# Four graph-attention layers over 16 graphs: adjacency masks as transposed byte pairs, and another order of the first and last layers

## The chip, the cores and the metric

The kernel runs on one core of one Trainium2 chip. The metric is device time in microseconds from start to end of one execution; the median of five runs is given with the lowest and the highest. The profile is of one further execution.

## The reference, cut to what matters

There are 16 graphs of 1024 nodes with 256 features, and for each a symmetric adjacency of 1024 x 1024 int32 (0 or 1, the diagonal set). Four attention layers follow each other, each on the normalised, rectified features, each added to the features:

```python
h = jnp.maximum(_layernorm(x, axis=-1), 0.0)
x = x + _L0_gnn_ref(h, adj, W, a)          # layers 1, 2 and 3 alike, with weights of their own

# _L0_gnn_ref, 4 heads of 64:
h = (x @ W).reshape(Bq, Nq, H, HD).transpose(0, 2, 1, 3)
s1 = jnp.einsum('bhnd,hd->bhn', h, a1)
s2 = jnp.einsum('bhmd,hd->bhm', h, a2)
e = jax.nn.leaky_relu(s1[:, :, :, None] + s2[:, :, None, :], 0.2)
e = jnp.where(adj[:, None, :, :] == 0, -jnp.inf, e)
out = jnp.einsum('bhnm,bhmd->bhnd', jax.nn.softmax(e, axis=-1), h)
```

Layers 0 to 2 have four heads; layer 2 also adds a bias, rectifies, adds its own `h` and normalises each head (gamma, beta). Layer 3 has one head of 256.

## The kernel before

`tile_gnn_stack_kernel` runs `fast_path` and then a general path, which is entered only if a check at the end of the fast path found data outside its assumptions (adjacency entries other than 0 and 1 among them). For the data of this case only the fast path does the work, and all that follows is about it.

**The work on a tile.** The exponential of a leaky ReLU of a sum is written as a product of factors and a maximum, so that it needs no exponential for each pair of nodes. The factors are made once for a layer (`fac`). A tile is one head and one block of 128 neighbours j against all 1024 nodes. For each tile ACT computes `r = relu(scale * rows + bias)` into PSUM (`weigh`; `rows` holds a factor of all 1024 nodes, the same on each partition), DVE computes `p = (r + base) * mask` into SBUF (`cover`, a scalar_tensor_tensor with the uint8 mask), and PE sums `po += p^T v` with `v` the projected features and a column for the denominators (`gather`, 16 matmuls for each half of the nodes). `ps_r` has two buffers of 128 x 1024 float32, there are TILES = 12 buffers for `p`, and two for `po`. With four heads and eight blocks a layer ("unit") has 32 tiles; there are 48 such units, named (graph, layer) below. Layer 3 is handled by `last_layer` and `last_sums`: 16 halves of two blocks each by ACT and DVE, then 8 blocks of sums on PE, each followed by an output transfer from `y`.

**Around a unit.** `prepare` takes the statistics (`st` on DVE, `rs` on POOL), `normal` scales the features (`hn` on POOL), turns them on PE and rectifies them (`hT`, ACT), `project` multiplies by the weights (`wa`) and copies the result (`v`, ACT). Then come the greatest scores (`mx`, `top`, `diag`, `c`), the factors (`fac`), and `rows`: the factor is turned on PE, copied by DVE (`row`), written to DRAM by SP (`line`), and read back to all partitions once for each head (`rows`, or `rows_one` for layer 3). There are ROWS = 3 buffers, so a row is requested when the head three places earlier has been weighed. After the sums, `evacuate` takes `po` to `att` and `finish` scales it, for layer 2 adds the bias and normalises, and adds it to `x_cur`, all element-wise steps on POOL and reductions on DVE.

**The masks.** `load` brings a graph's features (SP, one transfer) and its adjacency. For graphs 0 and 1 (TURNED = 2) `fetch` casts blocks of 128 rows to bf16 on their way into SBUF (issued by POOL), PE transposes them, ACT squares the result into the mask with a sum (`edges`), and PE sums the untransposed block. For the other 14 graphs POOL issues four casting transfers of 256 rows each from int32 to bf16 in DRAM (`near`), and SP then eight transposing transfers, one for each block of 128 columns, into two `raw` buffers. For each block `far_edges` has ACT go over `raw` twice: once to square it into the uint8 mask, once to copy it, each with a sum. At the end the two kinds of sums are compared; they are equal only if all entries are 0 or 1.

**The order.** Instructions are issued under a manual schedule. The planner (`while True` at line 1180) keeps a time for each engine (`Plan`, with costs of its own), offers the next `weigh`, `cover` and `gather` and all open jobs (generators that yield the engine of their next step and a condition), and on the engine that is free first takes, among what is ready within NEAR = 60 ns of the earliest, what is due first. Each engine then runs its instructions strictly in that order, SP its transfers too. The order of units is a rule (line 1129): it interleaves the graphs so that a unit is normally at least two places behind the one whose result it needs. It ends (13,2), (14,1), (15,0), (14,2), (15,1), (15,2). Loads begin EARLY = 110 tiles ahead of a graph's first unit, and layer 3 of a graph half a unit after its layer 2 has begun.

**The start.** Before the planner's loop, SP issues the transfers of all weights and attention vectors, DVE folds the vectors into the weights (16 products and 16 reductions), and only then do the planner's instructions begin on SP and DVE.

Of the kernel before, what the change touches and what calls it, by code (L numbers as in the profile page):

```python
# [9 lines left out]
F32 = mybir.dt.float32  # L10
BF16 = mybir.dt.bfloat16
I32 = mybir.dt.int32
# [364 lines left out]
TURNED = 2  # L377
# [10 lines left out]
M_PE = 300.0  # L388
# [10 lines left out]
LARGE = ("v_", "x_cur", "mask", "sums", "greatest", "p0", "p1", "p2", "p3", "p4", "p5", "p6", "p7", "p8", "p9", "r_", "po", "pl", "pp", "row", "hT", "raw", "inv")  # L399
# [81 lines left out]
def fast_path(  # L481
# [39 lines left out]
    NQ = NB // QUAD  # L521
# [11 lines left out]
    ident_b = const.tile([P, P], BF16, name="ident_b")  # L533
    make_identity(nc, ident_b)
# [6 lines left out]


    sums = const.tile([P, 2, G * NB], F32, name="sums")

    ones_b = const.tile([P, 1], BF16, name="ones_b")
    nc.vector.memset(ones_b, 1.0)

    def rows(src: bass.AP, offset: int, dims: list, name: str, pool, **kw):

        t = pool.tile([P] + [n for _, n in dims], F32, name=name, **kw)  # L550
        nc.sync.dma_start(t, bass.AP(tensor=src.tensor, offset=src.offset + offset, ap=[[0, P]] + dims))
        return t
# [3 lines left out]
    for k in range(KC):  # L556
        f = slice(k * P, (k + 1) * P)
        nc.sync.dma_start(wa[0][:, k, :, :HO], w_0[f, :].rearrange("p (h e) -> p h e", h=H))
        nc.sync.dma_start(wa[1][:, k, :, :HO], w_1[f, :].rearrange("p (h e) -> p h e", h=H))
        nc.sync.dma_start(wa[2][:, k, :, :HO], w_2[:, f, :].rearrange("h p e -> p h e"))  # L560
    with (
        tc.tile_pool(name="fold", bufs=2) as prep,
        tc.tile_pool(name="ps_w", bufs=2, space=bass.MemoryType.PSUM) as ps_w,
    ):
        w3_in = prep.tile([P, KC, F], F32, name="w3_in", bufs=1)
        nc.sync.dma_start(w3_in, w_3.rearrange("(c p) f -> p c f", p=P))
        for k in range(KC):
            pw = ps_w.tile([P, 512], F32, name="pw")
            for c in range(KC):
                nc.tensor.transpose(pw[:, c * P : (c + 1) * P], w3_in[:, c, k * P : (k + 1) * P], ident)  # L570
            nc.vector.tensor_copy(wa[3][:, k, 0, :F], pw[:, :F])
        for side in range(2):
            r = [
                rows(a_0, side * HO, [[2 * HO, H], [1, HO]], "a0", prep),
                rows((a_src_1, a_dst_1)[side], 0, [[HO, H], [1, HO]], "a1", prep),
                rows((a_src_2, a_dst_2)[side], 0, [[T * HO, H], [1, HO]], "a2", prep),
                rows(a_3, side * F, [[F, 1], [1, F]], "a3", prep),
            ]
            for layer in range(LAYERS):
                w = F // HEADS[layer]  # L580
                for k in range(KC):
                    prod = prep.tile([P, HEADS[layer], w], F32, name=f"prod{HEADS[layer]}")
                    nc.vector.tensor_mul(prod, wa[layer][:, k, :, :w], r[layer])
                    nc.vector.tensor_reduce(wa[layer][:, k, :, w + side], prod, AX.X, ALU.add)
    bias_r = rows(bias_2, 0, [[1, F]], "bias_r", const)
    gamma_r = rows(gamma_2, 0, [[1, F]], "gamma_r", const)
    beta_r = rows(beta_2, 0, [[1, F]], "beta_r", const)
# [7 lines left out]
    ps_r = ctx.enter_context(tc.tile_pool(name="ps_r", bufs=2, space=bass.MemoryType.PSUM))  # L595
# [23 lines left out]

    def load(g: "Graph"):  # L620

        yield "SP", lambda: (g.b < LIVE or layers[g.b - LIVE][0].g.done) and (
            g.b == 0 or layers[g.b - 1][0].g.loaded
        )
        g.x = graphs.tile([P, NB, F], F32, name="x_cur")
        sp.dma_start(g.x, x[g.b].rearrange("(c p) f -> p c f", p=P))
        g.here = plan.now
        g.mask = graphs.tile([P, NB, N], U8, name="mask")
        if g.b < TURNED:
            for nb in range(2):  # L630
                yield "POOL", None
                fetch(g, nb)
            return
        near = dram.tile([N, N], BF16, name="near", bufs=1)
        for k in range(0, N, N // 4):
            yield "POOL", None
            pool.dma_start(near[k : k + N // 4, :], adj[g.b, k : k + N // 4, :])
        there = plan.now + FETCH
        for j in range(NB):
            yield "SP", lambda: there if j < 2 else len(g.turned) > j - 2 and g.turned[j - 2]  # L640
            raw = work.tile([P, N], BF16, name="raw", bufs=2)
            sp.dma_start(raw, near[:, j * P : (j + 1) * P], transpose=True)
            add(g.until, far_edges(g, j, raw), plan.now)

    def far_edges(g: "Graph", j: int, raw: bass.AP):

        yield "ACT", None
        at = g.b * NB + j
        act.activation(g.mask[:, j, :], raw, AF.Square, accum_out=sums[:, 0, at : at + 1])
        g.left -= 1  # L650
        if not g.left:
            g.loaded = plan.now
        yield "ACT", None
        act.activation(raw, raw, AF.Copy, accum_out=sums[:, 1, at : at + 1])
        g.turned.append(plan.now)

    def fetch(g: "Graph", nb: int):
        raw = work.tile([P, N], BF16, name="raw", bufs=2)
        pool.dma_start(raw, adj[g.b, nb * P : (nb + 1) * P, :])
        add(g.until, edges(g, nb, raw), plan.now)  # L660

    def edges(g: "Graph", nb: int, raw: bass.AP):

        yield "PE", free_bank
        at = g.b * NB + nb
        pt, k = bank(BF16)
        for j in range(NB):
            pe.transpose(pt[:, j * P : (j + 1) * P], raw[:, j * P : (j + 1) * P], ident_b)
        yield "ACT", None
        act.activation(  # L670
            g.mask[:, :, nb * P : (nb + 1) * P],
            pt.rearrange("p (j n) -> p j n", j=NB),
            AF.Square,
            accum_out=sums[:, 0, at : at + 1],
        )
        drop(k)
        g.left -= 1
        if not g.left:
            g.loaded = plan.now
        yield "PE", free_bank  # L680
        pc, k = bank()
        for j in range(NB):
            pe.matmul(pc[:, 0:1], raw[:, j * P : (j + 1) * P], ones_b, start=(j == 0), stop=(j == NB - 1))
        yield "DVE", None
        dve.tensor_copy(sums[:, 1, at : at + 1], pc[:, 0:1])
        drop(k)
        if nb + 2 < NB:
            yield "POOL", None
            fetch(g, nb + 2)
# [27 lines left out]
    def project(e, i: int):  # L717

        u = e.u
        width = u.n * (u.w + 2)  # L720
        yield "PE", free_bank
        pv, slot = bank()
        for k in range(KC):
            for c in range(0, P, P // 2):
# [565 lines left out]
```

## Time and profile before

| what | value |
|---|---|
| median of 5 runs | 3102.45 us (3101.4 to 3104.15) |
| the profiled execution | 3100.49 us, span 3098.5 us, mean granted clock 0.972 |
| PE busy, idle | 2756.0 us (89%), 342 us |
| DVE busy | 2636.0 us (85%) |
| ACT busy | 2526.8 us (82%) |
| POOL busy | 1596.5 us (52%) |
| DMA queues, share of 16 engines | 20.2% (SP's), 5.5% (POOL's) |

A page gives the busy time of each engine, the span in 40 slices of about 77 us, and the costliest groups of instructions: engine, operation, output <- inputs, number, then busy time with the mean of one, then the idle time of that engine just before them and what ended it. All instructions of the planner bear line 459, a helper's, so groups are told apart by their tiles. PE is matrix multiplication, PEld its weight loads (they overlap), SP issues transfers. A busy PE need not be at its peak, since the ends of matmuls are modelled. Idle time on an engine costs something only where the others wait too.

### The profile page before, as it was taken

The page shows a single profiled execution, that of the slowest core. Times are in us where ns is not written, and L with a number is a line of the kernel's source. Part 1 is how long each engine was busy: PE and PEld are TensorE (multiplying, and loading weights), DVE is VectorE, ACT ScalarE, POOL GpSimd, SP SyncE. Part 2 cuts the span into 40 slices and gives each one's busy share as a digit, 9 for nine tenths or more (in the row PEclk, how much of TensorE's full clock was granted, in tenths as well). Part 3 has the DMA queues.
Part 4 walks back from the last instruction along what each step waited for, and adds up shares of the span by engine and source line. Part 5 has one row for each costly group of instructions (what it writes and reads, how often), then busy time and mean ns, then how long its engine had stood idle before and what let it go on. Part 6 is the DMA issues. An engine that isn't in the chain of part 4 may idle for free.

```text
span 3098.5 us, 130601 instructions
## 1 busy us (share of the span) xinstructions
PE 2756.0 (89%) x58885; PEld 2259.7 (73%) x58885; DVE 2636.0 (85%) x4062; ACT 2526.8 (82%) x3425; POOL 1596.5 (52%) x2288
## 2 busy tenths in 40 slices
PE   3889899899899989999899999989999999999875
PEld 2777677778787777778777777877777777777663
DVE  2878999788898989899898989989898898999672
ACT  2889898887979798897979889897988979887652
POOL 2433765463654727555372655637365463745441
PEclk8999999999999999999999999999999999999997
DMA  4331311413242331323224132321313232111010
GB/s 114 84 81 48 94 54 56 96 54 84 69 107 55 86 78 50 88 69 102 57 66 93 55 88 69 89 69 59 89 57 97 61 91 76 42 42 53 19 43 22
DMA packets 197079, 217.35 MB, mean 70 GB/s; under 512 B 131360, under 2 KB 166944, under 8 KB 195616
## 3 DMA queue, kind: packets, MB, share of 16 engines
q1 hardware_dynamic: 192416, 175.35, 20.2%
q0 software_dynamic: 4096, 33.56, 5.5%
q8 instruction: 463, 7.59, 1.0%
q14 instruction: 104, 0.85, 0.1%
HBM read 195.43 MB, written 46.99 MB: 78 GB/s over the span
## 4 chain that ended last, share of the span: by engine, by line
ACT 36%; DVE 25%; PE 23%; issue 7%; POOL 4%; DMA 4%; SPq 0%; DVEq 0%; ACTq 0%; POOLq 0%
ACT r L459 24%; DVE p L459 15%; PE pp L459 12%; PE po L459 11%; ACT mask L459 3%; ACT raw L459 3%; ACT v L459 2%; ACT hT L459 2%; DVE att L459 2%; DMA raw<-near 2%; DVE st L459 2%; POOL rs L459 2%; DVE s L459 1%; ACT att L459 1%; POOL hn L459 1%
## 5 line engine op out<-in xcount | busy, mean ns | idle before, releaser
L459 ACT ACTIVATE r<-rows,fac 128x1024 f32<-128x1024 f32 x1536 | 1754.3, 1154 | 291.9 <-DVE p L459 278.2
L459 PE MATMUL po<-v,p 128*64 128x65 f32 x49152 | 1667.7, 226 | 195.2 <-DVE p L459 124.1
L459 PEld LDWEIGHTS po<-v,p 128*64 128x64 f32 x49152 | 1586.0, 140 | 341.8 <-DVE p L459 135.2
L459 DVE SCALAR_TENSOR_TENSOR p<-r,mask 128x1024 f32<-128x1024 f32 x1024 | 1222.9, 1218 | 188.4 <-ACT r L459 146.2
L459 DVE SCALAR_TENSOR_TENSOR p<-r,fac,mask 128x1024 f32<-128x1024 f32 (+1 forms) x768 | 817.5, 1099 | 70.2 <-ACT r L459 62.8
L459 PE MATMUL pp<-wa,hT 128*64 128x264 f32 (+1 forms) x4096 | 528.9, 392 | 9.4 <-ACT v L459 5.0
L459 POOL TENSOR_TENSOR att<-att,inv 128x512 f32<-128x512 f32 x128 | 133.5, 1043 | 722.8 <-DVE inv L459 678.4
L459 PE MATMUL pp<-v_one,p 128*64 128x257 f32 x4096 | 491.0, 383 | 12.4 <-DVE p L459 10.1
L459 PEld LDWEIGHTS pp<-v_one,p 128*64 128x64 f32 x4096 | 284.4, 138 | 136.0 <-issue 11.7
L459 PEld LDWEIGHTS pp<-wa,hT 128*64 128x64 f32 x4096 | 267.1, 138 | 143.0 <-ACT v L459 13.0
L459 POOL TENSOR_SCALAR hn<-x_cur,rs 128x256 f32<-128x256 f32 x512 | 282.3, 566 | 21.8 <-PE pp L459 17.7
L459 PE MATMUL pp<-ident,hn 128*128 128x128 f32 x1024 | 184.6, 300 | 86.3 <-POOL hn L459 65.7
L459 POOL TENSOR_TENSOR x_cur<-att,x_cur 128x512 f32<-128x512 f32 x192 | 227.7, 1186 | 15.1
L459 ACT ACTIVATE r<-rows_one,fac 128x512 f32<-128x512 f32 x256 | 198.1, 780 | 33.9 <-DVE p L459 18.4
L459 PEld LDWEIGHTS pp<-ident,hn 128*128 128x128 f32 x1024 | 112.0, 146 | 146.2 <-POOL hn L459 107.8
L459 DVE BATCH_NORM_STATS2 st<-x_cur 128x6 f32<-128x256 f32 x512 | 179.1, 409 | 18.2 <-DMA x_cur<-in_x_dram 9.9
L459 ACT ACTIVATE hT<-pp 128x512 f32<-128x512 f32 x256 | 149.6, 595 | 50.7 <-PE pp L459 49.3
L459 POOL TENSOR_TENSOR att<-att,bias_r 128x512 f32<-128x512 f32 x64 | 75.8, 1185 | 181.8 <-DVE att L459 104.3
L459 ACT COPY v<-pp 128x264 f32<-128x264 f32 x384 | 142.8, 383 | 29.9 <-PE pp L459 28.1
L459 POOL TENSOR_TENSOR v<-v,fac 128x512 f32<-128x512 f32 x128 | 140.1, 1115 | 29.6 <-ACT fac L459 29.6
L459 POOL TENSOR_TENSOR att<-att,s 128x512 f32<-128x512 f32 x128 | 133.5, 1043 | 10.3
L459 ACT ACTIVATE mask<-raw 128x1024 uint8<-128x1024 bf16 x112 | 117.4, 1048 | 19.2 <-DMA raw<-near 19.2
(83 smaller groups left out, 1637.2 us busy)
## 6 DMA issues: line engine op xcount, KB each, us to landing
rows<-line SPq DMA_DIRECT2D x192, 512.0 KB, 4.0
near<-in_adj_dram POOLq DMA_DIRECT2D x56, 512.0 KB, 8.5
x_cur<-in_x_dram SPq DMA_DIRECT2D x16, 1024.0 KB, 9.7
out_dram<-y SPq DMA_DIRECT2D x128, 128.0 KB, 1.8
rows_one<-line SPq DMA_DIRECT2D x16, 512.0 KB, 4.1
raw<-in_adj_dram POOLq DMA_DIRECT2D x16, 256.0 KB, 4.4
raw<-near SPq DMA_TRANSPOSE x112, 3.7
wa<-in_L_gnn_W_dram SPq DMA_DIRECT2D x6, 128.0 KB, 7.1
```

Source lines behind the costliest of these rows:

```text
L459: r = call(*a, **k)
```

## The change

What it does:

- The adjacency is cast from int32 to uint8 in DRAM (four transfers a graph, one for each 256 nodes), and the bytes are taken two at a time as a 16-bit element, so that four transposing transfers bring a whole graph into SBUF: partition p holds the nodes 2p and 2p + 1 of each 256. They go straight into `g.edges`; the mask of block j is every second byte. Nodes are permuted accordingly in the loads of x and in the output.
- ACT no longer makes the masks. All graphs take this way; the path over PE for graphs 0 and 1 is gone.
- The check reads the int32 adjacency again, 8 pieces of 128 x 1024 a graph, and ACT goes over each once, with `(a - 0.5)^2` summed: 0.25 for each 0 or 1 (`looked_over`, `look`).
- Weights are loaded and folded as jobs of the planner, layer by layer (`weights`), behind graph 0's features. The first unit may also use the wide PSUM buffers for its preparation, and its first head's `rows` are made by 16 matmuls on PE and one copy (`direct`); the same for graph 15's layer 3.
- The last nine units get an order written out. Layer 3 of graph 13 is held until 100 tiles before the end of all tiles (HOLD). The last unit's heads 2 and 3 are finished on DVE (BY_DVE = 2). Graph 15's layer 3 sums its first four blocks side by side in four PSUM buffers.
- Some copies may go to either ACT or DVE; with DVE_MORE = 1e9 they go to ACT. The planner's margin after PE (M_PE) goes from 300 to 400 ns.

The core of the diff:

```diff
-TURNED = 2
+BY_DVE = 2
+HOLD = 100
+DVE_MORE = 1e9
+DIRECT = 1
+DELAY = 12000.0
...
-M_PE = 300.0
+M_PE = 400.0
...
+    def weights(layer: int):
+
+        yield "SP", lambda: layers[0][0].g.x is not None and (DELAY * layer + 1.0)
+        p, slot = numerators()
...
+        for c in range(2):
+            sp.dma_start(a[:, c], rows(*vectors[c]))
...
+        for c in range(2):
+            for k in range(KC):
+                yield "DVE", lambda: landed
+                dve.tensor_mul(prod, wa[layer][:, k, :, :w], a[:, c])
+                dve.tensor_reduce(wa[layer][:, k, :, w + c], prod, AX.X, ALU.add)
+        leave(slot, 2)
+        folded[layer] = plan.now
...
-        sp.dma_start(g.x, x[g.b].rearrange("(c p) f -> p c f", p=P))
+        sp.dma_start(
+            g.x.rearrange("p (q c) f -> p q c f", c=2), x[g.b].rearrange("(q p c) f -> p q c f", p=P, c=2)
+        )
         g.here = plan.now
-        g.mask = graphs.tile([P, NB, N], U8, name="mask")
...
-        near = dram.tile([N, N], BF16, name="near", bufs=1)
-        for k in range(0, N, N // 4):
+        g.edges = graphs.tile([P, NQ2, N], BF16, name="mask")
+        near = dram.tile([N, N // 2], BF16, name="near", bufs=2)
+        to = near.bitcast(U8).rearrange("(q c p) m -> q c p m", c=2, p=P)
+        of = adj[g.b].rearrange("(q p c) m -> q c p m", p=P, c=2)
+        for q in range(NQ2):
             yield "POOL", None
-            pool.dma_start(near[k : k + N // 4, :], adj[g.b, k : k + N // 4, :])
+            pool.dma_start(to[q], of[q])
         there = plan.now + FETCH
-        for j in range(NB):
-            yield "SP", lambda: there if j < 2 else len(g.turned) > j - 2 and g.turned[j - 2]
-            raw = work.tile([P, N], BF16, name="raw", bufs=2)
-            sp.dma_start(raw, near[:, j * P : (j + 1) * P], transpose=True)
-            add(g.until, far_edges(g, j, raw), plan.now)
...
+        for q in range(NQ2):
+            yield "SP", lambda: there
+            sp.dma_start(g.edges[:, q, :], near[:, q * P : (q + 1) * P], transpose=True)
+        g.loaded = plan.now + 3000.0
+        add(g.until + 2 * STEPS, looked_over(g), plan.now)
+
+    def looked_over(g: "Graph"):
+
+        of = adj[g.b].rearrange("(p r) m -> p (r m)", p=P)
+        for k in range(0, N * N // P, N):
+            yield "SP", lambda: len(looks) < 2 or (looks[-2] or False)
+            raw = work.tile([P, N], I32, name="raw", bufs=2)
+            sp.dma_start(raw, of[:, k : k + N])
+            looks.append(None)
+            add(g.until + 2 * STEPS, look(raw, len(looks) - 1), plan.now)
+
+    def look(raw: bass.AP, k: int):
         yield "ACT", None
-        at = g.b * NB + j
-        act.activation(g.mask[:, j, :], raw, AF.Square, accum_out=sums[:, 0, at : at + 1])
...
-        act.activation(raw, raw, AF.Copy, accum_out=sums[:, 1, at : at + 1])
...
+        act.activation(raw, raw, AF.Square, bias=-0.5, accum_out=sums[:, k : k + 1])
+        looks[k] = plan.now
+
+    def mask(g: "Graph", j: int, at: slice = slice(None)):
+
+        e = g.edges[:, j // 2, :].bitcast(U8).rearrange("p (n c) -> p n c", c=2)
+        return e[:, at, j % 2]
...
+        direct = u is main[0] or n == 1 and u.g.b >= G - DIRECT
+        if direct:
+
+            yield "PE", free_wide
+            pr, k = wide_bank()
+            for b in range(NB):
+                for m in range(0, P, P // 2):
+                    of = u.fac[:, 0, 0, b : b + 1].to_broadcast([P, P // 2])
+                    pe.matmul(pr[m : m + P // 2, b * P : (b + 1) * P], of, ident)
+            yield "DVE", None
+            over = units.tile([P, N], F32, name="rows", bufs=ROWS)
+            dve.tensor_copy(over, pr)
...
-            dve.scalar_tensor_tensor(p, r, base, u.g.mask[:, j, :], ALU.add, ALU.mult)
+            dve.scalar_tensor_tensor(p, r, base, mask(u.g, j), ALU.add, ALU.mult)
...
+        eng, name = (dve, "DVE") if u is main[-1] and h >= H - BY_DVE else (pool, "POOL")
...
+        if u is layers[-1][-1]:
+
+            yield "PE", lambda: there(0) and all(opened) and all(t is not None for t in banks) and max(there(0), *banks, *opened[-2:])
+            free = [bank(), bank(), (ps_o.tile([P, 512], F32, name="po"), None), (ps_o.tile([P, 512], F32, name="po"), None)]
...
+    if G > 5:
+
+        b = G - 4
+        order = [(b, 2), (b + 1, 1), (b + 2, 0), (b + 3, 0), (b + 1, 2), (b + 2, 1), (b + 3, 1), (b + 2, 2), (b + 3, 2)]
+        main[-9:] = [layers[i][k] for i, k in order]
...
+                if b >= G - 2:
+                    u.held = main[b - G - 1] if len(main) > 2 else None
+                if b == G - 3:
+                    u.gate = len(main) * STEPS - HOLD
...
+    for layer in range(LAYERS):
+        begins.append((-(10**6), weights(layer), turn[0, min(layer, 2)] + (layer > 2) * STEPS - 5 * STEPS // 4))
```

## The prediction

> **What bounds the kernel now.** I read the page first: busy shares, slices, costliest groups.
>
> ```profile
> PE 2756.0 (89%) x58885; PEld 2259.7 (73%) x58885; DVE 2636.0 (85%) x4062; ACT 2526.8 (82%) x3425; POOL 1596.5 (52%) x2288
> ...
> PE   3889899899899989999899999989999999999875
> ```
>
> No engine is the bound alone: three of them are within 230 us of each other, and a tile passes from ACT (`r`) to DVE (`p`) to PE (`po`) through only two `r` buffers. So time goes where one engine makes the next one wait, and where there is too little to do: the first slice has PE at 3 tenths and the last at 5. Next I asked for busy time by stretches, for the two ends beside a middle stretch.
>
> ```profile
> 1500.00:1800.00 300.00, 281.10 (x6039) 230.13 (x6037) 271.11 (x414) 260.00 (x350) 171.00 (x233) 0.99 0.28 74
> ...
> 2900.00:2950.00 50.00, 34.60 (x444) 23.04 (x438) 20.04 (x56) 20.49 (x40) 12.55 (x25) 0.89 0.12 39
> ```
>
> Columns after the length: PE, PEld, DVE, ACT, POOL busy, clock, DMA share, GB/s. In the middle DVE is busy 90%; in 2900 to 2950 only 40%. Then the waits between 300 and 2880 us, and the operations by form:
>
> ```profile
> DVE p L459 <- ACT r L459: 157.6, 263, 3.5
> ...
> L459 ACT ACTIVATE raw<-raw 128x1024 bf16<-128x1024 bf16 x112 | 117.5, 1049 | 0.6
> L459 ACT ACTIVATE mask<-raw 128x1024 uint8<-128x1024 bf16 x112 | 117.4, 1048 | 19.2 <-DMA raw<-near 19.2
> ```
>
> DVE waits 158 us for `r` in the middle, and ACT spends 235 us (with its accumulator reads, 191 ns each, 278) on the two passes a mask block. To see whether these are linked I went through the timeline of ACT and DVE and put each idle time of DVE that ended with an `r` under "edge" when a mask or raw pass lay in it or ended within 1.2 us before it: 79 us of the 158 us, in 88 of 263 waits. The last view is the timeline, at the start and the end:
>
> ```profile
> 26.06 0.38 SPq L459 DMA_DIRECT2D x_cur<-in_x_dram  x1
> 31.43 2.71 DVE L459 BATCH_NORM_STATS2 st<-x_cur 128x6 f32<-128x256 f32 x8 [5.45 <-DMA x_cur<-in_x_dram]
> 57.00 0.27 DVE L459 TENSOR_REDUCE mx<-v 128x8 f32<-128x64 f32 x1 [5.66 <-ACT v L459]
> 69.52 2.15 ACT L459 ACTIVATE r<-rows,fac 128x1024 f32<-128x1024 f32 x2 [2.30 <-DMA rows<-line]
> ...
> 3024.08 2.71 DVE L459 BATCH_NORM_STATS2 st<-x_cur 128x6 f32<-128x256 f32 x8 [6.01 <-POOL x_cur L459]
> 3043.04 0.18 DVE L459 TENSOR_REDUCE mx<-v_one 128x2 f32<-128x16 f32 x1 [16.26 <-ACT v_one L459]
> 3051.56 10.82 ACT L459 ACTIVATE r<-rows_one,fac 128x512 f32<-128x512 f32 x14 [5.25 <-DMA rows_one<-line]
> ```
>
> The first `r` comes at 69.5 us. The loads of the weights stand first on SP and their folding first on DVE, so graph 0's features are requested only at 26 us. At the end the last graph's fourth layer runs alone: 89 us from its last `po` sum at 3010 to 3099, in which PE is busy 50.
>
> **The change, part by part.** The sum is against the profiled execution, 3100.5 us (span 3098.5); the median of the runs is 3102.5.
>
> *Edge passes.* ACT loses 224 passes with their reads, 224 x (1.05 + 0.19) = 278 us, and 16 PSUM ones, 16 x 1.21 = 19; it gains 128 `look` passes over int32. No row shows ACT reading int32; the same size from bf16 is 1.05 and from f32 rows into PSUM 1.15, plus 0.19: 1.24 to 1.34 each, 159 to 172 us. I take 1.24, since source and target lie in SBUF as in the bf16 row: ACT is 138 us lighter. Little of that is on the path; what is, are the DVE waits. Half as many passes should leave half of the 79 us: **-40**. Ends: 0, if each look costs what two passes cost now, and -79, if looks only fill idle time. They have a later due time (two units after the masks), but ACT is picked by who is ready first, so a look starts in any gap over 60 ns and can still hold back an `r`; hence the middle.
>
> *The wait at 174 us.* ACT sits 9.2 us behind a mask pass whose transposed block has not landed (175 to 183 us, DVE and PE empty too). Masks no longer pass through ACT, and DVE needs that one some 100 tiles later: **-8** (0 to -9).
>
> *Head.* SP now issues graph 0's features first. They landed in 5.3 us alone and in 12.2 beside other traffic; with 4 MB of adjacency moving beside them I take 10: statistics at 11 instead of 31.4. From `st` to `mx` took 25.6 us here, with edge work between, and 19.0 undisturbed (3024.1 to 3043.0): `mx` at 30. Layer 0's four weight loads queue behind x and fold in 4 x 0.84 = 3.4 us of DVE while POOL normalises, hidden; if they land 10 us late, they cost that much. `mx` to `fac` 4.2, then 16 matmuls and one 1.1 us copy in place of the trip through DRAM (61.9 to 69.5 now): about 3. First `p` at 38 to 39, not 70.7: -32. But DVE also needs the mask, which before came through PE in pieces: four casts (a middle batch kept the DMA engines busy from 1261 to 1276, 15 us), then four transposes of 3.7 us to landing, so 34 us alone and 44 with x and weights beside. I take 44: **-25**, ends 0 and -32.
>
> *Order of the last units.* Now (15,1) is followed at once by (15,2), which needs its result: DVE does 16.2 of 45 us between 2905 and 2950 where 89% would be 40. With (14,2) between them this goes: **-20** (0 to -24).
>
> *The end.* Heads 2 and 3 of the last unit finish on DVE: seven operations of 1.04 to 1.19 us on POOL become about 0.7 to 0.86 (DVE's `att` rows of 512): -3. Rows by matmul instead of line and rows_one (3046.6 to 3051.6): -3. Four blocks summed side by side instead of in turn: PE stays at 256 x 0.109 = 28 us, so -2. The fourth layers of graphs 13 and 14 are held back to fill the gap: such a layer is some 17 us of DVE (16 x 0.74 and 8 x 0.65), which leaves the full stretch; part of it lies there already (64 `pp` matmuls at 3009.7): **-10** (0 to -19). Together **-18**.
>
> *At nothing.* The mask read with a step of two bytes: `p` is 1218 and 1277 ns for 1024 elements with a step of one; the row with a wide step, `mx<-v`, takes 259 ns for 64 elements, `top` 269 for 128. I take 0. If it cost 5%, 1792 x 0.06 = 107 us would eat the gain; no reason excludes that, and none speaks for it. Loads of int32 for the looks: 128 x 512 KB; a 1 MB load took 5.3 us, so about 2.6 us each, 340 us of all engines, while 48 transposes go; a DMA share near 26% goes to 30%. They are covered by rows being requested two heads ahead. On SP, each issue is 0.3 us and the wait for a free `raw` stands before rows, as transposes did before. The larger PE margin moves the whole order: +-15.
>
> Sum: 40 + 8 + 25 + 20 + 18 = 111; 3100.5 - 111 = 2989.5, about **2992** on the scale of the median.
>
> *A rule against it.* The row: a batch of casts, each 256 rows in one run, kept about 0.8 of the 16 DMA engines busy for 15 us, 48 engine-us each. The Trainium skill ("DMA: Bandwidth & Descriptors", Why a DMA increments its semaphore by 16 and not by 1) says that a transfer is spread over the largest count up to 16 that divides the slowest dimension of both patterns; the new source pattern begins with a dimension of 2, so by the page two engines would carry each cast. By an estimate from that, a cast takes 24 us; if the four take different pairs the masks come 10 us later at the start (2999), if they share one pair, 96 us, and the second rival below holds. No row here shows such a pattern.
>
> **The rivals.** *First: only the ends gain.* Looks fall into the same places as the passes did, and graph 0's mask comes as late as 70 us: 3100.5 - 8 - 38 = 3054. For it: ACT idles 258 us in the middle behind DVE, and a 1.24 us look fits into few of these gaps (365 of them, 0.7 us mean). Against it: half the passes are gone.
>
> *Second, slower: SP is held by the casts.* The four transposes stand on SP 15 us after the casts were planned and wait there in order; behind them are `rows`, `line`, x and the output. A row is requested two heads ahead; a graph takes 182 us for its 12 heads, so 30 us, less 4.0 to landing: 26 us of cover. So nothing happens until a batch takes 15 + 26 = 41 us; beyond that each graph from the third on loses the rest, 14 times. At 49 us the gain is gone; at 60 us it is 14 x 19 = 266, and with -111 gives 3256. Against: 15 us in the row, with less to write now (1 MB, not 2).
>
> *Third: the passes are not the cause.* If DVE's waits near mask passes go to other ACT work, and the tail order meets a new wait, gains and the 107 us of a slower mask read cancel: within 6 us of 3102.
>
> **How the numbers follow.** The forecast (2940 to 3040) has 0.68; the first rival (3040 to 3090) 0.18; the second 0.09; the third 0.03; still faster, with all upper ends (3100 - 179 = 2921), 0.02. The range 2940 to 3075 takes in the first rival's 3054 and a bit beyond, and leaves out under 0.2. 0.2% (6 us) is about what this kernel's measurement can tell from no change; so faster 0.88, same 0.03, slower 0.09.
>
> **What would show it.** Right: first `r` at 36 to 45 us; ACT busy near 2390; DVE's wait for `r` near 115 in the middle; `p` still 1.22 and 1.28 us; no stretch of 45 us after 2800 with DVE under half before the last unit ends; 64 transposes. Wrong: ACT `r` waiting for `rows`, SP waiting long for `near`, `p` above 1.3 us, or DVE waiting on transposed masks at the start.

## The result, and the profile after

The changed kernel takes 3109.79 us (median of 32 runs, 3099.64 to 3119.51) against 3102.59 us before (54 runs, 3094.97 to 3110.21). The ratio is 1.0021, 95% interval 1.0015 to 1.0027: slower by 0.2%, where 111 us less were forecast. The profiled execution took 3111.57 us, its span is 3109.7, so 11.2 us more span than before.

The page after, with the rows that answer to those of before. The last two columns of a DMA row are the size of one transfer and the median time from its issue to its landing; a queue's row has packets, MB and share.

```profile
PE 2764.9 (89%) x58692; PEld 2258.5 (73%) x58692; DVE 2645.5 (85%) x4062; ACT 2415.5 (78%) x3201; POOL 1609.7 (52%) x2262
...
PE   3879789899998999899999989999999989989867
...
q0 software_dynamic: 132096, 17.24, 7.9%
...
L463 ACT ACTIVATE raw<-raw 128x1024 int32<-128x1024 int32 x128 | 134.9, 1054 | 57.2 <-DMA raw<-in_adj_dram 56.9
...
near<-in_adj_dram POOLq DMA_DIRECT2D x64, 256.0 KB, 27.0
```

ACT's busy time is 111 us lower (the times of its instructions add up to 142 us less, where 138 were forecast), and DVE's work is the same, but nothing got shorter by it. The row to notice is the last: a cast lands after 27.0 us. Before it was this, for twice the bytes written:

```profile
q0 software_dynamic: 4096, 33.56, 5.5%
...
near<-in_adj_dram POOLq DMA_DIRECT2D x56, 512.0 KB, 8.5
```

The two stretches after (columns as before):

```profile
1500.00:1800.00 300.00, 280.74 (x5862) 226.81 (x5862) 270.16 (x416) 247.15 (x325) 160.64 (x223) 0.99 0.31 84
2900.00:2950.00 50.00, 43.98 (x1106) 39.47 (x1104) 48.79 (x71) 34.91 (x30) 32.22 (x33) 0.97 0.17 55
```

The lull at 2900 is gone (DVE 48.8 of 50, before 20.0). In the middle ACT is busy 13 us less and DVE 1 us less: no more tiles went through. DVE's wait for `r` between 300 and 2880 us rose:

```profile
DVE p L463 <- ACT r L463: 181.0, 247, 7.1
```

Sorted as in the prediction, the part beside mask or check passes fell from 79 to 54 us, and the rest rose from 79 to 127.

The start, from the timelines of DVE, ACT and PE (start, length, and in brackets the idle time before and what ended it):

```profile
16.48 0.43 DVE L463 TENSOR_TENSOR p<-wa,p 128x256 f32<-128x256 f32 x1 [15.45 <-DMA p<-in_L_gnn_a_dram]
...
24.11 2.70 DVE L463 BATCH_NORM_STATS2 st<-x_cur 128x6 f32<-128x256 f32 x8
...
44.12 0.27 DVE L463 TENSOR_REDUCE mx<-v 128x8 f32<-128x64 f32 x1 [9.38 <-ACT v L463]
...
52.93 2.15 ACT L463 ACTIVATE r<-rows,fac 128x1024 f32<-128x1024 f32 x2 [3.97 <-DVE rows L463]
...
82.21 1.06 ACT L463 ACTIVATE raw<-raw 128x1024 int32<-128x1024 int32 x1 [20.89 <-DMA raw<-in_adj_dram]
...
75.89 0.66 PE L463 MATMUL pp<-ident,p 128*128 128x128 f32 x2 [15.39 <-DMA p<-in_L_gnn_W_dram]
```

The statistics wait behind the fold of layer 0, and the fold for `a_0` until 16.5 us. The first `r` comes at 52.9 instead of 69.5, but soon all engines stand: ACT's look has no data until 82 us, and PE's transposes of the layer 3 weights none until 76.

The end:

```profile
3008.43 0.42 DVE L463 BATCH_NORM_STATS2 st<-x_cur 128x6 f32<-128x256 f32 x1
...
3036.87 0.18 DVE L463 TENSOR_REDUCE mx<-v 128x2 f32<-128x16 f32 x1 [16.62 <-ACT v L463]
...
3023.86 2.30 PE L463 MATMUL pp<-ident,hn 128*128 128x128 f32 x8 [10.67 <-POOL hn L463]
...
3055.65 1.13 PE L463 MATMUL pp<-v,p 128*64 128x257 f32 x4 [5.80 <-DVE y L463]
```

Graph 15's statistics begin 101 us before the end (before: 74). They are spread over 3008 to 3020, in one piece of 2.7 us before, since graph 14's held layer 3 is interleaved with them; then PE waits 10.7 us for `hn` as if nothing had been held back.

**A ruler.** Each four-head unit has one `mx`, and the first 39 units come in the same order in every kernel here. The start of the 13th and of the 39th `mx`, read from DVE's timeline, cut each span into three parts: the start with the first units, 26 units of steady work (nearly nine graphs), the end. Each row is one execution. `after` and `oldtail` issue the same instructions until past the 39th `mx`, and their first two parts still differ by 4 and 5 us (`cast16` and `c16_oldtail`: 2 and 2), so differences of that size in this table say nothing.

| kernel | to 13th `mx` | 13th to 39th | 39th to the end | span |
|---|---|---|---|---|
| before | 769.2 | 1552.8 | 776.4 | 3098.5 |
| after | 770.3 | 1567.3 | 772.1 | 3109.7 |
| cast16 | 735.6 | 1543.4 | 764.7 | 3043.7 |
| after_c16first | 759.3 | 1565.7 | 771.1 | 3096.2 |
| before_2eng | 778.6 | 1628.0 | 788.9 | 3195.5 |
| onepass | 754.0 | 1561.6 | 784.1 | 3099.7 |
| nolook | 736.5 | 1557.1 | 774.5 | 3068.0 |
| oldtail | 766.4 | 1562.1 | 774.5 | 3103.0 |
| c16_oldtail | 737.9 | 1545.8 | 769.0 | 3052.8 |
| c16_nolook | 726.1 | 1521.5 | 766.6 | 3014.2 |
| c16_loadonly | 729.3 | 1521.6 | 766.5 | 3017.4 |
| c16_look2 | 744.0 | 1552.0 | 756.7 | 3052.6 |
| c16_mpe300 | 736.7 | 1543.6 | 752.6 | 3032.9 |
| before_mpe400 | 765.4 | 1549.3 | 773.6 | 3088.3 |
| c16_head | 721.1 | 1541.6 | 763.6 | 3026.3 |
| c16_head300 | 727.7 | 1543.4 | 752.2 | 3023.3 |
| c16_h2s | 737.8 | 1543.3 | 764.7 | 3045.8 |
| c16_best | 730.0 | 1543.7 | 765.6 | 3039.3 |

### The profile page after: what moved, and what is told of

It is laid out like the page before. It is cut to its first block, busy times and chain, and to the rows that moved or that the text cites. A ratio compares the mean times of both kernels' runs of the same rounds, so it can differ in the third digit from the quotient of the medians.

```text
span 3109.7 us, 130089 instructions
## 1 busy us (share of the span) xinstructions
PE 2764.9 (89%) x58692; PEld 2258.5 (73%) x58692; DVE 2645.5 (85%) x4062; ACT 2415.5 (78%) x3201; POOL 1609.7 (52%) x2262
## 3 DMA queue, kind: packets, MB, share of 16 engines
q0 software_dynamic: 132096, 17.24, 7.9%
## 4 chain that ended last, share of the span: by engine, by line
PE 32%; DVE 25%; ACT 18%; DMA 12%; POOL 5%; issue 5%; SPq 1%; ACTq 0%; POOLq 0%; DVEq 0%
PE pp L463 19%; DVE p L463 16%; ACT r L463 14%; PE po L463 13%; DMA near<-in_adj_dram 5%; DMA raw<-in_adj_dram 4%; DVE st L463 2%; DVE att L463 2%; POOL rs L463 2%; ACT raw L463 2%; SPq L463 1%; POOL hn L463 1%; ACT v L463 1%; DVE s L463 1%; DMA line<-row 1%
## 5 line engine op out<-in xcount | busy, mean ns | idle before, releaser
L463 ACT ACTIVATE r<-rows,fac 128x1024 f32<-128x1024 f32 (+1 forms) x1552 | 1765.4, 1148 | 330.5 <-DVE p L463 318.1
L463 PE MATMUL po<-v,p 128*64 128x65 f32 x49216 | 1685.5, 226 | 185.0 <-DVE p L463 85.9
L463 DVE SCALAR_TENSOR_TENSOR p<-r,mask 128x1024 f32<-128x1024 f32 x1024 | 1220.8, 1217 | 159.6 <-ACT r L463 131.8
L463 PE MATMUL pp<-v_one,p 128*64 128x257 f32 x3584 | 434.5, 381 | 1.6 <-issue 0.7
L463 PEld LDWEIGHTS pp<-v_one,p 128*64 128x64 f32 x3584 | 242.9, 137 | 99.4 <-issue 1.5
L463 ACT ACTIVATE r<-rows_one,fac 128x512 f32<-128x512 f32 x240 | 186.6, 782 | 32.2 <-DMA rows_one<-line 11.3
L463 ACT COPY v<-pp 128x264 f32<-128x264 f32 (+1 forms) x395 | 146.5, 381 | 53.8 <-PE pp L463 53.2
L463 ACT ACTIVATE raw<-raw 128x1024 int32<-128x1024 int32 x128 | 134.9, 1054 | 57.2 <-DMA raw<-in_adj_dram 56.9
```

Source lines behind the costliest of these rows:

```text
L463: r = call(*a, **k)
```

## The experiments

### The order of the casts' dimensions

**cast16**: both patterns of the cast name the 128 pairs first and the two rows of a pair second; the same bytes go to the same places, the instructions of all engines are the same.

```diff
-        to = near.bitcast(U8).rearrange("(q c p) m -> q c p m", c=2, p=P)
-        of = adj[g.b].rearrange("(q p c) m -> q c p m", p=P, c=2)
+        to = near.bitcast(U8).rearrange("(q c p) m -> q p c m", c=2, p=P)
+        of = adj[g.b].rearrange("(q p c) m -> q p c m", p=P, c=2)
```

> The changed kernel with one edit: both patterns of the cast are written p c m instead of c p m, so that they begin with 128 and not with 2; the same bytes go to the same places. Theory A (each cast is carried by two of the 16 DMA engines: 27.0 us to landing against 8.5 before, DMA share 0.55 to 0.60 for some 25 us while only the casts run): the casts land in under 15 us, the first p comes at 40 to 46 us instead of 54, the stop from 62 to 82 us shrinks to under 8 us, and the kernel takes 3075 to 3090. Theory B (casts are slow because each is 2064 packets of 130 bytes, whatever the order of dims): landing stays above 20 us and the time within 5 us of the changed kernel's. Theory C (the planner's order eats what the ends give): casts land early, but the time stays within 8 us.

Measured: 3046.0 us (3045.6 to 3051.6), ratio to before 0.9826 (0.9813 to 0.9839). A cast lands after 9.5 us:

```profile
q0 software_dynamic: 17408, 16.78, 6.1%
...
near<-in_adj_dram POOLq DMA_DIRECT2D x64, 256.0 KB, 9.5
```

How many engines carry a cast is seen where four of them run and hardly another transfer is under way (after, then cast16; the last columns are the DMA share and GB/s):

```profile
1293.00:1297.00 4.00, 3.08 (x88) 2.83 (x82) 2.38 (x14) 1.46 (x3) 0.30 (x2) 1.00 0.55 83
1297.00:1301.00 4.00, 3.45 (x96) 3.01 (x95) 3.27 (x9) 0.75 (x2) 1.31 (x2) 1.00 0.58 56
```

```profile
1240.00:1244.00 4.00, 4.00 (x48) 2.45 (x46) 2.84 (x3) 4.00 (x8) 0.00 (x0) 1.00 1.12 108
```

0.55 to 0.58 of 16 engines is about what four transfers on two engines each would show (8 of 16, and a little else); the reordered casts keep all of them busy (a share over 1 means that the times of packets overlap). The rival that smaller packets are the cause (theory B gives them 130 bytes) falls with the trace's records of single packets: in both kernels the casts' data goes in 16384 packets of 1 KB, with a median of 173 ns each; the 114688 further packets of after hold 4 bytes each. What differs is how many data packets run at a time, 6.1 on average after and 14.6 in cast16 (the casts of graph 8). So this one order cost the changed kernel 64 us, twice what theory A allowed it; the first `p` came at 52 us though, not at 40 to 46, since the fold and the weights still stood in its way.

**before_2eng**: the kernel before, only with such an order (even rows, then odd rows, same places).

```diff
-            pool.dma_start(near[k : k + N // 4, :], adj[g.b, k : k + N // 4, :])
+            to, of = near[k : k + N // 4, :], adj[g.b, k : k + N // 4, :]
+            to, of = (e.rearrange("(p c) m -> c p m", c=2) for e in (to, of))
+            pool.dma_start(to, of)
```

> The kernel before, with only the order of the cast's dimensions changed: each of its four transfers a graph names even rows first and odd rows second, same bytes to the same places. Theory A (a pattern that begins with a dimension of 2 is carried by two of the 16 DMA engines): landing of near rises from 8.5 us to 20-30 us in the middle, and the time by 10 to 40 us (3112 to 3142), most of it at the first graph that takes this way (graph 2) and a little in each later batch. Theory B (the dear part of the new transfer is its one-byte target, not the order of dimensions): landing stays within 2 us of 8.5 and the time within 5 us of 3102.

Measured: 3197.5 us (3190.6 to 3200.9), ratio 1.030 (1.0286 to 1.0314): 95 us slower, more than twice the most that theory A allowed, and 75 of it in the middle part, 8 to 9 us a graph.

```profile
L459 ACT ACTIVATE mask<-raw 128x1024 uint8<-128x1024 bf16 x112 | 117.5, 1049 | 95.7 <-DMA raw<-near 95.7
...
near<-in_adj_dram POOLq DMA_DIRECT2D x56, 512.0 KB, 27.0
```

The one-byte target is not the cause (theory B); the landing is the same 27.0 with two-byte elements. Of the mechanism the first row tells most: ACT, in order, stood 95.7 us before mask passes whose block had not come, against 19.2 before, 5 to 6 us more for each of the 14 graphs.

**after_c16first**: the changed kernel, the casts' dimensions reordered for graphs 0 and 1 only.

```diff
+        d = "q p c m" if g.b < 2 else "q c p m"
```

> The changed kernel with the casts' dimensions reordered for graphs 0 and 1 only. Theory S (slow casts cost at the start, where masks, weights and looks wait for the same engines, and little later, since a graph's masks come 100 tiles ahead): 3070 to 3085, that is 25 to 40 of the 64 us. Theory T (they cost evenly, in all 16 batches): 3098 to 3106.

Measured: 3098.3 us (3094.1 to 3106.5), ratio 0.999 (0.998 to 1.0): in the range of theory T, but the cost is not as even as that theory says. The first two graphs are worth 11 of the 64 us. Set beside cast16 by the starts of `mx`, after_c16first then loses 20 us with graphs 2 and 3 (up to 380 us), and some 3 us with each of the twelve later ones. With these two graphs its ACT stands 5.6 and 6.3 us before looks whose load has not landed (150 to 217 and 283 to 380 us; in the same units of cast16 1.2 and none); over the whole span such waits are 56.9 us after and 37.9 in cast16. Later, with after set beside cast16 (their instruction orders are equal), the lead is flat within a graph and grows at each batch of casts: 42.0 us at 1198, 44.2 at 1329, 47.2 at 1508, 52.0 at 1690 (times of cast16). What happens there, first after, then cast16 (SP, ACT and PE; a batch was issued at 1276.8 and at 1234.8):

```profile
1301.85 0.33 SPq L463 DMA_DIRECT2D rows_one<-line  x1
1309.22 5.21 SPq L463 DMA_TRANSPOSE mask<-near  x4
...
1308.34 1.60 ACT L463 ACTIVATE r<-rows_one,fac 128x512 f32<-128x512 f32 x2 [2.38 <-DMA rows_one<-line]
...
1305.92 1.85 PE L463 MATMUL po<-v,p 128*64 128x65 f32 x54 [1.63 <-issue]
```

```profile
1255.71 0.33 SPq L463 DMA_DIRECT2D rows_one<-line  x1
1256.20 6.48 SPq L463 DMA_TRANSPOSE mask<-near  x4
...
1263.00 1.60 ACT L463 ACTIVATE r<-rows_one,fac 128x512 f32<-128x512 f32 x2 [0.21 <-DVE p L463]
```

Nobody waits for the masks themselves; they come 100 tiles ahead. But the read of a row falls into the long tail of the casts: `rows_one` lands after 6.6 us (median from 300 to 2880 us), 4.2 with short casts, and ACT stands for it. And PE stands for nothing that the profile names ("issue"): between 300 and 2300 us it has 15 such gaps of 0.8 us or more after, 11 of them (14.5 us) within 40 us of a batch; cast16 has 4 and none there, before 5 and 2, before_2eng 13 and 11. A queue named "instruction" shares the DMA engines (462 packets, 1.0%), so code that comes late would look like this; that it is code was not shown, nor how the 24 us of the middle divide between rows, looks and these gaps.

### ACT's passes

**onepass**: the kernel before without the second of the two passes over each block of `raw` (`far_edges`), so that one of the two sums is not made: 112 x 1.24 = 139 us less of ACT.

```diff
-        yield "ACT", None
-        act.activation(raw, raw, AF.Copy, accum_out=sums[:, 1, at : at + 1])
```

> The kernel before, with the second pass of ACT over each transposed block left out (the plain sum is not made and the comparison of the two sums compares a sum with itself); 112 passes of 1.24 us less, 139 us of ACT, and nothing else is edited. This is the part of the change that the forecast priced at 40 us, alone. Theory A (half as many passes take away half of the waits beside them): DVE's wait for r from 300 to 2880 us falls from 158 to about 118, and the time by 30 to 50 us, to 3052 to 3072. Theory C (ACT's load is not what makes DVE wait; the order is): the wait stays above 145 and the time within 12 us of 3102.

Measured: 3098.7 us (3095.7 to 3104.9), ratio 0.9988 (0.9978 to 0.9998). 3 us for 139. DVE's wait for `r` from 300 to 2880 us is 143.5 us (157.6 before), and sorted as in the prediction the part beside passes fell only from 79 to 67. By the ruler 15 us shorter at the start and 16 longer behind it: another order, no more.

**nolook**: the changed kernel without the check of the adjacency's entries, neither its loads nor its passes.

```diff
-        add(g.until + 2 * STEPS, looked_over(g), plan.now)
```

> The changed kernel without the check of the edges: no loads of the int32 pieces, no passes of ACT over them; the sums are set to the value that the check expects. ACT is 160 us lighter than in the changed kernel. Theory A (passes of ACT hold back r: 54 us of DVE's 181 us of waits in the middle lie beside a look): DVE's wait for r in the middle falls to 130 to 145 and the time by 35 to 55 us, to 3055 to 3075. Theory C (DVE waits for r whenever ACT's in-order queue meets something late, and the planner fills what is freed with other work): DVE's wait stays above 165 and the time falls by less than 20 us, most of it at the start, where ACT stood 21 us behind a look's load.

Measured: 3069.9 us (3068.3 to 3072.4), ratio 0.9898 (0.9884 to 0.9913), 40 us below after; DVE's wait for `r` from 300 to 2800 us is 126 us (after 176). By the ruler 34 of the 40 lie before the 13th `mx`, where looks and weights compete with casts and ACT stands before an empty `raw`; 10 in the middle. Theory A's time and wait came true, but not the place that it gave for them.

**c16_nolook** is the same with the casts' dimensions reordered.

> The changed kernel with the casts' dimensions reordered, and without the check of the adjacency's entries (no loads of int32, no passes on ACT). Theory C (ACT's passes cost nearly nothing in the middle, since the planner puts other work into the gaps): 3030 to 3042, most of the gain before 100 us where a look stops ACT for 15 us, under 8 us from 100 to 2900 us. Theory F (ACT's 160 us of passes stand on the path there as the prediction had it): 3000 or less, with the gain spread evenly over the middle.

Measured: 3020.6 us (3016.0 to 3026.9), ratio 0.9737 (0.9724 to 0.975), 25 us below cast16. Neither theory: the middle gives 22 us, nearly three times what C allowed, and far less than the 160 us of passes.

**c16_look2** makes a second pass over each block (`act.activation(raw, raw, AF.Copy)` ahead of the first), 135 us more of ACT.

> The changed kernel with the casts' dimensions reordered, and a second pass of ACT over each block of the check (128 x 1.05 = 135 us more on ACT). Leaving the looks out gave 25 us. Theory P (a pass of ACT in the middle costs a sixth of its length, as leaving out 160 us for 25 us says): 3064 to 3076. Theory Q (the price is the loads and the start; ACT's passes fall into gaps, as leaving out 139 us in the old kernel for 3 us says): 3044 to 3054.

Measured: 3054.9 us (3050.3 to 3059.4), ratio 0.9848 (0.9832 to 0.9863): 9 us above cast16, with 8 in each of the first two parts, and the end 8 shorter. Theory Q missed by 1 us, P by 9.

**c16_loadonly** keeps the int32 loads and leaves out the passes, so that nothing is checked.

```diff
-            looks.append(None)
-            add(g.until + 2 * STEPS, look(raw, len(looks) - 1), plan.now)
+            looks.append(plan.now)
```

> The changed kernel with the casts' dimensions reordered; the int32 loads of the check are kept, ACT's passes over them left out (so nothing is checked). Its engines' order is that of c16_nolook, 3020.6. Theory U (the loads are the price: 64 MB on the same DMA engines as rows, x and masks): 3036 to 3048. Theory V (the passes are the price): 3018 to 3026.

Measured: 3021.2 us (3019.2 to 3023.0), ratio 0.9741 (0.9727 to 0.9756), the same as without loads. So the traffic of 64 MB of loads costs nothing once the casts are short (theory V), and the passes, with what ACT waits for in front of them, cost what there is: 25 us for 160, and 9 for a further 135. The rows of the looks in cast16 and in c16_look2:

```profile
L463 ACT ACTIVATE raw<-raw 128x1024 int32<-128x1024 int32 x128 | 134.9, 1055 | 37.9 <-DMA raw<-in_adj_dram 37.9
...
L463 ACT ACTIVATE raw<-raw 128x1024 int32<-128x1024 int32 x256 | 269.3, 1053 | 11.5 <-DMA raw<-in_adj_dram 10.1
```

In cast16 ACT stood 37.9 us before looks whose load had not landed, in c16_look2 10.1; c16_nolook and c16_loadonly have no such wait. No run separates the passes from this standing. Together with onepass's 3 for 139 the price of a microsecond of ACT here is 0.02 to 0.16; how much of that is only the order that the planner deals is not shown.

### The order itself

**c16_mpe300** sets only the margin after PE back (`M_PE = 300.0`), **before_mpe400** sets it to 400 in the kernel before.

> The changed kernel with the casts' dimensions reordered, and the planner's margin after PE back at 300 ns: the same work in another order. Theory M (the order alone moves the time by no more than the prediction's 15 us): 3031 to 3061. Theory N (the order is the larger effect, so that single edits of 20 us can't be read from the total): further away than 15 us from 3046.

> The kernel before with the planner's margin after PE at 400 ns. Theory M (a larger margin is itself worse by about what it costs with reordered casts): 3108 to 3118. Theory N (it deals another order, luck of some 10 us in either direction): 3088 to 3104.

Measured: 3034.8 us (3033.6 to 3038.9), ratio 0.9782 (0.9769 to 0.9795), so 11 us below cast16, all of it after the 39th `mx`; and 3095.5 us (3089.6 to 3100.2), ratio 0.9978 (0.9969 to 0.9987), 6 us below before. The sign differs from kernel to kernel: no cost of the margin, but the luck of an order, about 10 us wide. Differences of that size between two kernels with different orders say nothing about an edit.

**oldtail** takes back the order of the last nine units, the holding of the fourth layers and their buffer; **c16_oldtail** does so with reordered casts.

```diff
-        main[-9:] = [layers[i][k] for i, k in order]
...
-                if b >= G - 2:
-                    u.held = main[b - G - 1] if len(main) > 2 else None
-                if b == G - 3:
-                    u.gate = len(main) * STEPS - HOLD
```

> The changed kernel with the old end: the order of the last nine units, the buffers and the holding back of the fourth layers of graphs 13 to 15 are as before; all else is the change. Theory A (the new order fills the lull but puts two fourth layers into the last 110 us, where PE has 64 blocks of matmuls to do one after another and the last graph's statistics stand between the other's p): the end from the last full tile is 90 to 100 us again instead of about 119, the lull before it is back, and the time is 3100 to 3112. Theory D (the new order is a gain and the loss is all at the start): 3125 to 3140.

> The changed kernel with the casts' dimensions reordered, and with the old order of the last units, the old hold of the fourth layers and their old buffer. Theory D (the prediction's term: the new order of the last units is worth about 20 us, the held layers 10): 3066 to 3076, against 3046 with the new end. Theory E (the new order fills the lull at 2905 to 2950 but pays it back when the last graph's statistics and layer meet the held layers): within 8 us of 3046.

Measured: 3115.0 us (3104.8 to 3123.2), ratio 1.0049 (1.0036 to 1.0061), and 3054.6 us (3050.6 to 3057.4), ratio 0.984 (0.9827 to 0.9854). Behind the 39th `mx` the new end saves 2.4 and 4.3 us, no more than equal instructions differ by, where 30 were forecast (the profiled execution of oldtail was its fastest, 10 us under its median). The first total lies between the two ranges expected of it; with the second theory E is at its edge (8.5 us in all, 4 by the ratios). The lull is filled, and the time comes back in the last 100 us.

### The start

**c16_head**: cast16, with the fold of layer 0 only after the first statistics, the weights of layers 2 and 3 at 60 and 120 us of the plan, and no look before 64 tiles.

```diff
-        yield "SP", lambda: layers[0][0].g.x is not None and (DELAY * layer + 1.0)
+        yield "SP", lambda: layers[0][0].g.x is not None and ((0.0, 12000.0, 60000.0, 120000.0)[layer] + 1.0)
...
-                yield "DVE", lambda: landed
+                yield "DVE", lambda: landed if layer or seen else False
...
-            yield "SP", lambda: len(looks) < 2 or (looks[-2] or False)
+            yield "SP", lambda: at_tile[0] >= 64 and (len(looks) < 2 or (looks[-2] or False))
```

> The changed kernel with the casts' dimensions reordered and three edits at the start: the fold of layer 0's weights only after the first statistics, the weights of layers 2 and 3 requested at 60 and 120 us of the plan and not at 24 and 36, and no look before 64 tiles are weighed. Theory G (the start is bound by transfers taken in too early an order): statistics at 10 to 14 us instead of 22, first p at 40 to 46 us instead of 52, the stop at 61 to 75 us gone, 3020 to 3030 in all. Theory H (graph 0's mask and graph 1's own transfers bound the start anyway, and the planner gives the rest back later): first p at 48 to 52, 3038 to 3048.

Measured: 3029.5 us (3024.4 to 3031.7), ratio 0.976 (0.9747 to 0.9774): theory G, and with c16_head300 the fastest kernel with all of its work, 2.4% under before. Which of the three edits did it is not separated; with them SP also asked for graph 1's features at 24.1 us instead of 53.6. The timeline of its DVE, and the stretch from 45 to 90 us in after, cast16 and c16_head:

```profile
6.36 2.71 DVE L463 BATCH_NORM_STATS2 st<-x_cur 128x6 f32<-128x256 f32 x8 [5.33 <-DMA x_cur<-in_x_dram]
...
33.43 0.27 DVE L463 TENSOR_REDUCE mx<-v 128x8 f32<-128x64 f32 x1 [7.70 <-ACT v L463]
```

```profile
45.00:90.00 45.00, 19.50 (x298) 17.98 (x299) 20.30 (x39) 14.15 (x19) 12.83 (x20) 0.59 0.72 159
```

```profile
45.00:90.00 45.00, 22.97 (x386) 20.07 (x387) 25.50 (x45) 22.87 (x34) 17.35 (x28) 0.70 0.71 167
```

```profile
45.00:90.00 45.00, 41.48 (x1029) 36.33 (x1027) 42.31 (x59) 37.96 (x50) 18.72 (x28) 0.97 0.62 124
```

DVE (the third time) works 42 of 45 us instead of 20 or 25. Of the 33 us that this leads cast16 by the 64th tile, nearly half is given back between 133 and 195 us, where the postponed weights and looks now come.

**c16_head300** is c16_head with `M_PE = 300.0`.

> The kernel of c16_head with the margin after PE back at 300 ns. Theory M (the two gains add): 3013 to 3023. Theory N (luck of the order): 3024 to 3040.

Measured: 3031.9 us (3025.2 to 3034.3), ratio 0.9776 (0.9762 to 0.979): no gain, so the two do not add. The end is 11 us shorter again, the first two parts 8 longer in the profile, which is 7 us under this kernel's median.

**c16_h2s** was to issue graph 0's casts after the first statistics and to ask for the weights of layers 1 and 2 later; **c16_best** adds a later due time of the looks.

```diff
-            yield "POOL", None
+            yield "POOL", lambda: g.b > 0 or bool(seen)
...
-        ... ((0.0, 12000.0, 60000.0, 120000.0)[layer] + 1.0)
+        ... ((0.0, 36000.0, 80000.0, 120000.0)[layer] + 1.0)
...
-            add(g.until + 2 * STEPS, look(raw, len(looks) - 1), plan.now)
+            add(g.until + 6 * STEPS, look(raw, len(looks) - 1), plan.now)
```

> The kernel of c16_head with graph 0's casts issued only after the first statistics and the weights of layers 1 and 2 requested at 36 and 80 us of the plan. Theory G (at the start the weights wait behind 4 MB of casts; the masks have 15 us to spare): layer 0's vectors land at 8 to 11 us instead of 18.6, first p at 32 to 37 us instead of 41.1, 3019 to 3026 in all. Theory R (the masks become the last to come): first p at 38 to 44 us, 3027 to 3034.

> The kernel of c16_h2s with the looks due six units after the masks instead of two, so that the planner takes other work of ACT first. Theory P (a look's price is that it stands in front of an r): 8 to 15 us below c16_h2s. Theory Q: within 6 us of c16_h2s.

Measured: 3046.1 us (3040.9 to 3048.3), ratio 0.981 (0.9795 to 0.9825), and 3040.4 us (3038.0 to 3041.7), ratio 0.9796 (0.9783 to 0.981). The first missed its aim, and so tells nothing about theories G and R: the condition orders the planner's time, but POOL had nothing to wait for in between, and the casts left at 1.5 us as ever. What changed was SP: graph 1's features were requested at 42.3 us instead of 24.1, and DVE stood 8.5 us for them; this need not be all of the 17 us, for c16_head300 asked for them as late (42.5). The second is 6 us below it, all at the start (theory Q), within the luck of an order.

## Why the prediction was wrong

**The rule that was weighed and left out of the sum held, and decided the sign.** The working had the rows (15 us a batch, 48 engine-us each) and the rule of the Trainium skill ("DMA: Bandwidth & Descriptors", Why a DMA increments its semaphore by 16 and not by 1), and from it an estimate of 24 us a cast. 27.0 were measured, 9.5 with the dimension of 128 first, and a DMA share of 0.55 to 0.58 for four under way. What failed was the next step, "masks come 10 us later at the start (2999)": it asked only who waits for the masks. The price was 64 us in the medians and 66 in the profiles: 35 to the 13th `mx`, 24 in the middle, 7 at the end (after minus cast16, by the table), where row reads and the looks' loads land later in the tail of a slow batch, and PE has gaps there. Of these, 11 us come from the first two graphs alone.

This step does not account for the whole: of the 118 us by which the forecast was off, 54 remain in cast16. It is 55 us of span under before, 34 to the 13th `mx`, 9 in the middle and 12 at the end, where 33 were forecast for the start, 40 for the edge passes and 38 for the end. That the start agrees is in part luck, since its first `p` came at 52 us and not at 44.

**Edge passes (-40).** The middle, 26 of 48 units, is 14.5 us longer after and 9.4 us shorter with reordered casts; 40 x 26/48 = 22 would have been its part. The step that failed is "half as many passes should leave half of the 79 us": the waits beside such passes did fall, from 79 to 54 (49 in cast16), but DVE's other waits for `r` rose from 78 to 127 (104 in cast16), and in onepass 139 us off ACT brought 3. Here a wait that ended with an engine was not the price of that engine's load.

**The wait at 174 us (-8) and the head (-25).** Right in kind, lost in after: first `p` at 54 instead of 70.7, then the stop from 62 to 82. Two steps failed. "Statistics at 11": they came at 24.1, for the fold stands before them and `a_0` landed at 16.5, with 4 MB of adjacency being cast beside it (that the casts held it up was not shown); the working took the fold as hidden behind POOL. And nothing asked what graph 1's casts, the looks and the layer 3 weights do to each other. c16_head repaired just this, with statistics at 6.4 and 48 us less than before to the 13th `mx`, and shows that the head could give what was forecast and more.

**The order of the last units (-20) and the end (-18).** The lull went as predicted, but the part after the 39th `mx` is 4.3 us shorter, not 38; taking the new end back costs 2.4 or 4.3. The step that failed is the sum of both. Work that fills the lull is taken from behind, and the last graph's chain from statistics to output, 74 us before, is longer now (101), with held layer 3 work between its steps.

**At nothing.** Right: `p` took 1217 and 1275 ns with the mask at a step of two bytes; a look 1054 + 196 ns, as taken; the loads cost nothing as traffic (c16_loadonly), though ACT stood before late ones. The +-15 for the margin was fair: 11 and 6 us were seen.

**The second rival** named the right object, casts that take longer than a batch should, but the wrong holder: SP does stand before the transposes (106 us in 25 waits), yet a batch took about 32 us, under its point of 41.

## What to carry to other kernels

Before an engine's saved time is priced, look at the transfers that come with it: here a pattern's first dimension cost more than the change saved, and others that share the DMA engines paid, though no engine waited for the masks themselves. Weigh such a rule by who else is on the queues, not only by who waits for the data. With an order dealt by a planner, change one margin first and see how far the time moves; no edit smaller than that can be read from a total, but landmarks of equal instructions can still tell where it lies, down to the 5 us by which two executions of the same instructions differ.

## What was not expected of the hardware

The same bytes to the same places took 27.0 us and 132096 packets with the dimension of 2 first, 9.5 us and 17408 packets with 128 first (the data packets are the same, the others hold 4 bytes), and the issue of a batch on POOL took 4.5 us instead of 3.0. The landing was 27.0 us as well with twice the bytes written (before_2eng). And PE's unnamed gaps of about 1.3 us came in the 20 to 40 us after the issue of a slow batch, and there hardly at all without one.
